# A graph layer on one core: sets of two units in a new order, 24 groups gathered wholly by TensorE, h's bf16 parts made by TensorE

## The chip, the core and the metric

One core of a Trainium2 chip. The metric is the device time of one execution in microseconds (us). The profile has one execution, with TensorE as PE (matmuls) and PEld (its weight loads), VectorE as DVE, ScalarE as ACT, GpSimd as POOL and the queues of DMA issues on SyncE as SPq.

## The reference: what is computed

```python
h = relu(layernorm(x))                       # x: 6250 nodes x 64
msg = relu(h[src] + edge_attr)               # 206250 edges x 64
agg = segment_sum(msg, dst, 6250)            # dst is sorted
out = x + (relu((h + agg) @ W1 + b1) @ W2 + b2)
```

The edges hold every drawn pair in both directions and one loop for each node, ordered by their destination.

## The kernel before

**Groups.** The 206250 edges are cut into 268 groups of 768 (6 columns of 128 edges) and a last, smaller one, numbered 268. Groups 0 to 4 are gathered wholly by GpSimd (`gather`, L204: one indirect DMA for each column of 128 rows). In the others GpSimd gathers three columns, and TensorE finds h for the other three; 12 groups (`WHOLE`) are found wholly by TensorE, in two halves. Three columns found by TensorE are a *unit*: 276 units, two to a *set*, 138 sets, and three sets to a round of ranks (46 rounds).

**How TensorE gathers.** h stands in SBUF as `hp`, 128 partitions x 49 rows x three bf16 parts x 64, whose sum is h. For each set the edges are sorted into places, at most 32 for each of 24 lists. `find` (L465, VectorE) compares the list of node numbers with each partition's number and writes `found`, a 0/1 matrix, in three comparisons (two over 1536 elements, one over 256). `slots_of` (L497, TensorE) multiplies `hp` by it, 52 matmuls of 128x32 weights for a unit, into three PSUM banks `half`, two columns of lists to a bank; `slots_out` (L506, ScalarE) copies a bank to `picked` in bf16. `back` (L484, VectorE; its last block by ScalarE, `back_far` and `back_near`, L474 and L477, as abs and relu of a difference) makes the 0/1 matrix `backs`, six blocks of 128x768 for a set. `pick` (L513, TensorE) multiplies it, 18 matmuls of 128x128 for a unit, and adds up in one of two `pick` banks, into which `room` (L522, ScalarE) has copied the unit's edge attributes.

**The rest of a unit.** `messages` adds the gathered columns (L597, VectorE), sums the three parts out of the `pick` bank (L600, VectorE) and applies relu (L602, ScalarE). `one_hot` (L581, VectorE) makes the matrix from each edge to the 32 destinations of the group's window. `window_sum` (L612, TensorE) multiplies the two, fp32, 128x64 weights, and `sum_into_z` (L575, VectorE) adds the result to z, which is transposed. Its column comes out of a register, loaded for 16 groups at a time by `window_start` (L442). `blocks_behind` starts the two matmuls with W1 and W2 (L631, L642) for every block of 512 nodes that is finished.

**Ranks.** The places come from counting: `rank_at` (L280, VectorE), `rank_count` (L285 and L287, TensorE, and L291, ScalarE), `rank_of` (L295 to L301, VectorE), `rank_marks`, `rank_turn` (L325, TensorE, L327, ScalarE), `rank_holds`, `rank_fits`, `source` (L339, TensorE, L344, ScalarE). The lists go to DRAM and come back to all partitions (`source_load`, `spot_load`).

**The order** is written by hand; nothing is rescheduled, each engine works through its instructions as `half(u)` and the code around it issue them. In `half(u)` a unit has TensorE's window sum of the unit before, the slots of the next set, and the pick of the next unit; then VectorE's and ScalarE's work, and one step of the ranks at certain units. Gathers of GpSimd wait for listed matmuls (`beats`), so that they come in time and not earlier.

**The start.** The layer norm goes through h in four pieces (`ln_head`, `ln_rows`), stores the rows for the gathers, and transposes them into z (`ln_turn`, L386, TensorE, L387, ScalarE). `ln_parts` makes the three parts of `hp` later, in steps that are put between the first groups' norms by `fill`: a cast by ScalarE (L392), a difference by VectorE (L394), a cast (L395), a difference (L397). `places` computes part and place numbers for all edges (L264 to L273, VectorE); `slots_of_edges` (L745 to L756) needs a matmul that spreads `base` (L747). Groups 0 to 2 are gathered from x itself and normed by `norm_edges` (L545 to L556).

## Time and profile before

| | |
|---|---|
| median of 3 runs (all) | 1082.63 us (1082.12, 1082.63, 1085.3) |
| profiled execution, its time | 1080.78 us |
| profiled execution, its span | 1079.1 us |
| mean granted TensorE clock | 0.974 |

The span reaches from the first to the last instruction; 1.7 us of the execution lie around it. Busy time counts an engine's own work, and a matmul's end has its drain in it, so successive matmuls overlap in the rows. "Idle before" is the engine's idle time in front of an instruction, with what ended it behind the arrow.

### The profile page before, as it was taken

To read this page: it belongs to the slowest core of one execution; us is meant where nothing else is said; L and a number is where in the kernel's file an instruction comes from. 1 tells how busy PE (TensorE), PEld (TensorE's weight loads), DVE (VectorE), ACT (ScalarE), POOL (GpSimd) and SP (SyncE) were. 2 spreads that over 40 slices of the span, in tenths; PEclk is the share of its full clock that TensorE was granted. 3 is DMA by queue.
4 is the path that set the end of the run, shared out by engine and by line. 5 is a ranking of instruction groups with operands and counts; after the bars stand their busy time and mean duration, and the time that the engine had idled before them with its cause. 6 is when DMAs were issued, how large, how long until landed. Compare 5 with 4: busy or idle time off the path is not lost.

```text
span 1079.1 us, 55140 instructions
## 1 busy us (share of the span) xinstructions
PE 994.9 (92%) x23185; PEld 865.5 (80%) x23185; DVE 960.5 (89%) x2686; ACT 940.6 (87%) x1979; POOL 793.9 (74%) x798
## 2 busy tenths in 40 slices
PE   3159999999999999999999999999999999999997
PEld 2148888888878888888888888888888888888885
DVE  8869889898998998998999898998999898998984
ACT  6459889899989998898998998998998998998985
POOL 7677777777777777777777777777777777777740
PEclk9659999999999999999999999999999999999998
DMA  6445566565655665665665656565656665655650
GB/s 207 126 117 150 164 164 187 141 178 158 188 143 150 180 190 143 170 169 165 163 174 149 184 157 165 155 199 156 161 148 187 164 170 154 185 158 161 167 132 10
DMA packets 115098, 172.36 MB, mean 160 GB/s; under 512 B 28444, under 2 KB 83613, under 8 KB 114845
## 3 DMA queue, kind: packets, MB, share of 16 engines
q1 hardware_dynamic: 89752, 143.03, 43.7%
q0 software_dynamic: 25088, 25.74, 13.5%
q8 instruction: 184, 3.01, 1.1%
q14 instruction: 70, 0.57, 0.2%
q10 hardware_dynamic: 4, 0.01, 0.0%
HBM read 164.85 MB, written 3.84 MB: 156 GB/s over the span
## 4 chain that ended last, share of the span: by engine, by line
PE 76%; DVE 10%; issue 5%; DMA 4%; ACT 3%; POOL 1%; DVEq 1%; SPq 0%; ACTq 0%
PE pick L513 34%; PE half L497 26%; PE half L612 10%; DVE backs L484 2%; DVE found L465 2%; DVE ea L600 2%; DMA xg<-h_rows,src_sb 2%; PE rows L339 2%; PE rows L642 1%; PE rows L631 1%; PE rows L287 1%; POOL xr L204 1%; DMA x<-in_x_dram 1%; DVE oh L581 1%; PE rows L285 1%
## 5 line engine op out<-in xcount | busy, mean ns | idle before, releaser
L204 POOL DMA_INDIRECT xg<-h_rows,src_sb x754 | 759.4, 1007 | 231.6 <-issue 105.2
L513 PE MATMUL pick<-picked,backs 128*128 128x192 bf16 x4968 | 459.9, 247 | 1.1 <-ACT pick L522 1.1
L513 PEld LDWEIGHTS <-backs 128*128 128x128 bf16 x4968 | 397.5, 98 | 45.1 <-issue 43.6
L506 ACT CAST picked<-half 128x384 bf16<-128x384 f32 x828 | 370.4, 480 | 54.3 <-PE half L497 47.2
L497 PE MATMUL half<-hp,found 128*32 128x192 bf16 x14352 | 352.8, 248 | 7.5 <-DVE found L465 4.9
L497 PEld LDWEIGHTS <-found 128*32 128x32 bf16 x14352 | 286.6, 97 | 22.2 <-issue 5.1
L484 DVE TENSOR_SCALAR backs<-spots,ids 128x768 bf16<-128x768 int16 x690 | 255.8, 419 | 0.0
L600 DVE TENSOR_REDUCE ea<-pick 128x192 f32<-128x576 f32 x276 | 206.8, 749 | 21.6 <-PE pick L513 19.7
L465 DVE TENSOR_SCALAR found<-sources,nodes_of 128x1536 bf16<-128x1536 int16 (+1 forms) x414 | 206.1, 525 | 0.1
L612 PEld LDWEIGHTS half<-oh,msg 128*64 128x64 f32 x3224 | 121.7, 138 | 62.0 <-issue 27.4
L522 ACT COPY pick<-ea 128x576 f32<-128x576 f32 x264 | 170.4, 646 | 0.0
L612 PE MATMUL half<-oh,msg 128*64 128x32 f32 x3224 | 152.4, 227 | 13.5 <-DVE z L575 10.8
L602 ACT ACTIVATE msg<-ea 128x384 f32<-128x384 f32 (+2 forms) x281 | 146.3, 521 | 10.7 <-DVE ea L600 7.2
L477 ACT ACTIVATE backs<-dist,ones 128x768 bf16<-128x768 bf16 x138 | 131.7, 954 | 0.3 <-ACT dist L474 0.3
L474 ACT ACTIVATE dist<-spots,far 128x768 bf16<-128x768 int16 x138 | 131.4, 952 | 0.0
L575 DVE TENSOR_TENSOR z<-z,half 128x32 f32 x281 | 50.9, 181 | 73.2 <-ACT picked L506 43.5
L581 DVE TENSOR_TENSOR oh<-slot,slots 128x192 f32<-128x192 int16 (+2 forms) x281 | 94.5, 336 | 1.0 <-PE half L612 1.0
L597 DVE TENSOR_TENSOR ea<-ea,xg 128x192 f32<-128x192 f32 x252 | 87.4, 347 | 0.7 <-issue 0.7
L285 PE MATMUL rows<-at,upper 128*128 128x432 f16 x46 | 16.4, 358 | 21.7 <-DVE at L280 19.7
L339 PE MATMUL rows<-holds,marks 128*96 128x96 f16 x276 | 25.8, 231 | 11.4 <-DVE holds L313 5.0
L291 ACT CAST before<-rows 128x432 f16<-128x432 f32 x46 | 23.9, 519 | 14.3 <-PE rows L287 14.3
L344 ACT CAST source<-rows 24x64 int16<-24x64 f32 x138 | 28.1, 203 | 9.5 <-PE rows L339 4.4
(107 smaller groups left out, 435.1 us busy)
## 6 DMA issues: line engine op xcount, KB each, us to landing
sources<-source_row SPq DMA_DIRECT2D x138, 384.0 KB
ea<-in_edge_attr_dram SPq DMA_DIRECT2D x268, 192.0 KB
spots<-spot_rows SPq DMA_DIRECT2D x138, 192.0 KB
xg<-h_rows,src_sb POOLq DMA_INDIRECT x754
xb<-in_x_dram SPq DMA_DIRECT2D x12, 128.0 KB
out_dram<-o SPq DMA_DIRECT2D x12, 128.0 KB
h_rows<-x SPq DMA_DIRECT2D x3, 384.0 KB
dst_sb<-in_dst_main_dram SPq DMA_DIRECT2D x1, 804.0 KB
```

The costliest lines, as they stand in the source:

```text
L204: it = nc.gpsimd.indirect_dma_start(out=xg[:, j, :], out_offset=None, in_=rows[:, :], in_offset=bass.IndirectOffsetOnAxis(ap=idx[:, j:j + ...
L465: nc.vector.tensor_scalar(found[k][:, b * PARTS:b * PARTS + n].rearrange("p m i s -> p (m i s)"), sources[k][:, :n * 2 * S], nodes_of[:, b ...
L474: nc.scalar.activation(dists[k], spots[k].bitcast(I16), AF.Abs, bias=far)
L477: nc.scalar.activation(backs[k][:, Q - 1].rearrange("p t s -> p (t s)"), dists.pop(k), AF.Relu, bias=ones[:, 0:1], scale=-1.0)
L484: nc.vector.tensor_scalar(backs[k][:, q].rearrange("p t s -> p (t s)"), spots[k].bitcast(I16), ids[:, q:q + 1], None, op0=ALU.is_equal)
L497: last = nc.tensor.matmul(ps[j * S:(j + 1) * S, u], found[k][:, m, i, :], hp[:, min(m, RR - 1)].rearrange("p t d -> p (t d)"), start=(b == ...
L506: nc.scalar.copy(picked[k][:, n0:n0 + 2], halves.pop((k, n0)))
L513: last = nc.tensor.matmul(ps[:, u, :3].rearrange("p t d -> p (t d)"), backs[k][:, q, i * H + u, :], picked[k][:, i * Q + q], start=False, ...
L522: nc.scalar.copy(picks[u][:, :H, :3], parts)
L600: nc.vector.tensor_reduce(ea[:, c0:c0 + H], picks.pop(u)[:, :H, :3].rearrange("p j t d -> p j d t"), AX.X, ALU.add)
L602: nc.scalar.activation(msg[:, lo:hi], ea[:, lo:hi], AF.Relu)
L612: last = nc.tensor.matmul(pa[i * D:(i + 1) * D], msg[:, j, :], oh[:, j, :], start=(j < lo + 2), stop=(j >= hi - 2))
```

## The change

- **Groups.** Every eleventh group from the tenth on is found wholly by TensorE: 24 for 12. There are 288 units, 144 sets, 48 rounds.
- **Order.** `half(u)` now differs for the first and the second unit of a set. The first issues the window sum, three banks of slots, the pick; the second the pick, three banks of slots, the window sum. The window sum of unit u-1 and that of u therefore follow each other on TensorE, and so do two picks (with a step of the ranks, or a result block, between them). `slots_out` directly follows each bank's slots. Both `sum_into_z` of a set stand in the first half, and the second `room` is issued there too. The steps of the ranks start one unit earlier.
- **Comparisons.** The third comparison of `found` is made by ScalarE (abs, then relu). The last block of `backs` is made by ScalarE for every other set and by VectorE for the rest; its two steps follow each other.
- **h's parts.** For each piece of the norm, TensorE multiplies h by the identity (fp32) and adds minus the first part (bf16) in a `pick` bank, ScalarE casts that to the second part; TensorE adds minus the second part, ScalarE casts the third. The transposes into z follow behind all pieces.
- **Smaller ones.** `code` is gone, its numbers are in `part`; the casts of `own` for all later rounds go to ScalarE, inside the norm; the norms of groups 0 to 2 go step by step for all three; `rank_of` of the third round is made in the start.

```diff
 F0 = 5
 SETS = 3
 RG = 2 * SETS
-HEAD, PERIOD = 2 * RG - 1, 4 * RG - 1
-assert (NG + 1 - F0 - HEAD) % PERIOD == 0
-WHOLE = [F0 + RG - 1] + list(range(F0 + HEAD + 2 * RG - 1, NG + 1, PERIOD))
+HEAD = PERIOD = 2 * RG - 1
+assert (NG + 1 - F0) % PERIOD == 0
+WHOLE = list(range(F0 + RG - 1, NG + 1, PERIOD))
 UNITS = []
 for g in range(F0, NG + 1):
     UNITS.append((g, G - H))
...
+    from_b = const.tile([P, PARTS, H], F16, name="from_b")
+    nc.gpsimd.iota(from_b, pattern=[[1, PARTS], [0, H]], base=BIAS // STEP, channel_multiplier=0,
+                   allow_small_or_imprecise_dtypes=True)
+    less_b = const.tile([P, P], BF16, name="less_b")
+    nc.vector.tensor_scalar_mul(less_b, ident, -1.0)
...
     def stretches(t_sb, c0, c1):
-        n, g0 = (HEAD, F0) if c0 == 0 else (PERIOD, F0 + HEAD + (c0 - 2) // 4 * PERIOD)
+        n, g0 = (HEAD, F0) if c0 == 0 else (PERIOD, F0 + c0 // 2 * PERIOD)
...
-    def places(c0, c1):
+    def places_own(c0, c1):
+        n = c1 - c0
+        own = lnp.tile([P, n, CC], F32, name="own", bufs=1)
+        m, parts = stretches(src_sb, c0, c1)
+        for src, w, gs in parts:
+            to = own.rearrange("p c s -> p (c s)").rearrange("p (e w g j) -> p e w g j", w=2, g=m, j=H)[:, :, w, gs]
+            if c0 == 0:
+                nc.vector.tensor_copy(to, src)
+            else:
+                nc.scalar.copy(to, src)
+        return own
+
+    def places(c0, c1, own):
         n = c1 - c0
         row = lnp.tile([P, n, CC], I16, name="row", bufs=1)
         off = lnp.tile([P, n, CC], F32, name="off", bufs=1)
         second = lnp.tile([P, n, CC], I16, name="second", bufs=1)
         third = lnp.tile([P, n, CC], F32, name="third", bufs=1)
-        own = lnp.tile([P, n, CC], F32, name="own", bufs=1)
-        m, parts = stretches(src_sb, c0, c1)
-        for src, w, gs in parts:
-            nc.vector.tensor_copy(own.rearrange("p c s -> p (c s)")
-                                  .rearrange("p (e w g j) -> p e w g j", w=2, g=m, j=H)[:, :, w, gs], src)
...
-        nc.vector.scalar_tensor_tensor(part[:, c0:c1], off, float(RR), third, op0=ALU.add, op1=ALU.add)
-        nc.vector.tensor_scalar(code[:, c0:c1], part[:, c0:c1], float(STEP), float(BIAS), op0=ALU.mult, op1=ALU.add)
+        nc.vector.scalar_tensor_tensor(part[:, c0:c1], off, float(RR + BIAS // STEP), third, op0=ALU.add, op1=ALU.add)
...
-        nc.vector.tensor_tensor(spot_i[c], ranks[c], code[:, c], ALU.add)
+        nc.vector.scalar_tensor_tensor(spot_i[c], part[:, c], float(STEP), ranks[c], op0=ALU.mult, op1=ALU.add)
...
                 nc.tensor.transpose(pt[:, u, :], h[:, i + u, :], ident[:PP, :PP])
             nc.scalar.copy(zv[:, :, r + i:r + i + n], pt[:, :n].rearrange("d u p -> d p u"))
-    def ln_parts(r, m, h):
+    def pieces(i, r, m):
+
+        flat = pick_banks[i % 2].rearrange("p j t d -> p (j t d)")
+        for a in range(0, m, 8):
+            b = min(a + 8, m)
+            yield flat[:, a * D:b * D], slice(a, b)
+
+    def mid_piece(i, r, m, h):
         hv = hp[:, r:r + m]
-        rest = lnp.tile([PP, m, D], F32, name="rest")
         nc.scalar.copy(hv[:, :, 0], h)
-        yield
-        nc.vector.tensor_tensor(rest, h, hv[:, :, 0], ALU.subtract)
-        nc.scalar.copy(hv[:, :, 1], rest)
-        yield
-        nc.vector.tensor_tensor(hv[:, :, 2], rest, hv[:, :, 1], ALU.subtract)
+        for ps, rows_of in pieces(i, r, m):
+            nc.tensor.matmul(ps, ident, h[:, rows_of].rearrange("p r d -> p (r d)"), start=True, stop=False)
+            nc.tensor.matmul(ps, less_b, hv[:, rows_of, 0], start=False, stop=True)
+        flat = pick_banks[i % 2].rearrange("p j t d -> p (j t) d")
+        nc.scalar.copy(hv[:, :, 1], flat[:, :m])
+
+    def low_piece(i, r, m, h):
+        hv = hp[:, r:r + m]
+        for ps, rows_of in pieces(i, r, m):
+            nc.tensor.matmul(ps, less_b, hv[:, rows_of, 1], start=False, stop=True, skip_group_check=True)
+        flat = pick_banks[i % 2].rearrange("p j t d -> p (j t) d")
+        nc.scalar.copy(hv[:, :, 2], flat[:, :m])
     def combine(xg, ea, n):
         nc.vector.tensor_tensor(xg[:, :n], xg[:, :n], ea[:, :n], ALU.add)
...
         nc.sync.dma_start(out=spots[k], in_=spot_rows[k * 2 * H:(k + 1) * 2 * H, :]
                           .rearrange("(o t) s -> o (t s)", o=1).to_broadcast([P, 2 * H * P]))
+    last_node = const.tile([P, 1], F32, name="last_node")
+    nc.vector.tensor_scalar_mul(last_node, nodes_of[:, BB:], -1.0)
+
     def find(k, b):
         if b == 0:
             found[k] = hot.tile([P, PARTS * BB + J, 2, S], BF16, name="found")
         n = PARTS if b < BB else J
-        nc.vector.tensor_scalar(found[k][:, b * PARTS:b * PARTS + n].rearrange("p m i s -> p (m i s)"),
-                                sources[k][:, :n * 2 * S], nodes_of[:, b:b + 1], None, op0=ALU.is_equal)
+        to = found[k][:, b * PARTS:b * PARTS + n].rearrange("p m i s -> p (m i s)")
+        if b < BB:
+            nc.vector.tensor_scalar(to, sources[k][:, :n * 2 * S], nodes_of[:, b:b + 1], None, op0=ALU.is_equal)
+        else:
+            dist = rank.tile([P, J * 2 * S], BF16, name="dist", bufs=1)
+            nc.scalar.activation(dist, sources[k][:, :n * 2 * S], AF.Abs, bias=last_node)
+            nc.scalar.activation(to, dist, AF.Relu, bias=ones[:, 0:1], scale=-1.0)
     far = const.tile([P, 1], F32, name="far")
     nc.vector.tensor_scalar_mul(far, ids[:, Q - 1:], -1.0)
-    dists = {}
+
+    def is_shared(k):
+        return k > 1 and k % 2 == 1
     def back_far(k):
-        dists[k] = rank.tile([P, 2 * H * P], BF16, name="dist", bufs=1)
-        nc.scalar.activation(dists[k], spots[k].bitcast(I16), AF.Abs, bias=far)
-
-    def back_near(k):
-        nc.scalar.activation(backs[k][:, Q - 1].rearrange("p t s -> p (t s)"), dists.pop(k), AF.Relu,
-                             bias=ones[:, 0:1], scale=-1.0)
+        to = backs[k][:, Q - 1].rearrange("p t s -> p (t s)")
+        apart = rank.tile([P, 2 * H * P], BF16, name="apart", bufs=1)
+        nc.scalar.activation(apart, spots[k].bitcast(I16), AF.Abs, bias=far)
+        nc.scalar.activation(to, apart, AF.Relu, bias=ones[:, 0:1], scale=-1.0)
+
+    def back_begin(k):
+        backs[k] = hot.tile([P, Q, 2 * H, P], BF16, name="backs")
     def back(k, q0, q1):
-        if q0 == 0:
-            backs[k] = hot.tile([P, Q, 2 * H, P], BF16, name="backs")
-        for q in range(q0, min(q1, Q - 1)):
+        if q0 == 0 and k not in backs:
+            back_begin(k)
+        for q in range(q0, min(q1, Q - is_shared(k))):
             nc.vector.tensor_scalar(backs[k][:, q].rearrange("p t s -> p (t s)"), spots[k].bitcast(I16),
                                     ids[:, q:q + 1], None, op0=ALU.is_equal)
         if q1 == Q:
...
-    def norm_edges(xg):
-        s = work.tile([P, G], F32, name="raw_s")
+    raw = {}
+
+    def raw_head(g):
+        xg = taken[g][1]
+        s = work.tile([P, G], F32, name="raw_s", bufs=RAW)
         nc.vector.tensor_reduce(s, xg, AX.X, ALU.add)
         nc.vector.tensor_scalar_mul(s, s, 1.0 / D)
         nc.vector.tensor_tensor(xg, xg, s.unsqueeze(2).to_broadcast([P, G, D]), ALU.subtract)
         sq = work.tile([P, G, D], F32, name="msg", bufs=3)
         nc.scalar.activation(sq, xg, AF.Square)
-        fill()
-        v = work.tile([P, G], F32, name="raw_v")
+        raw[g] = s, sq
+
+    def raw_var(g):
+        v, sq = raw[g]
         nc.vector.tensor_reduce(v, sq, AX.X, ALU.add)
         nc.scalar.activation(v, v, AF.Sqrt, bias=eps_sb, scale=1.0 / D)
-        fill()
+
+    def raw_rows(g):
+        xg, v = taken[g][1], raw.pop(g)[0]
         nc.vector.reciprocal(v, v)
         nc.vector.scalar_tensor_tensor(xg, xg, 0.0, v.unsqueeze(2).to_broadcast([P, G, D]),
                                        op0=ALU.max, op1=ALU.mult)
...
+    def slots_by(k, n0s):
+        for n0 in n0s:
+            last = slots_of(k, n0)
+            slots_out(k, n0)
+            if n0 != n0s[1]:
+                beats.append(last)
+
     def half(u):
         g = group_of(u)
         k, i = divmod(u, 2)
-        first = ((0, 2), (6, 8))[i]
-        later = ((4,), (10,))[i]
-        now = is_set(k + 1)
         if is_first(u):
             enter(g + AHEAD, beats[-G + H:])
+        if is_set(k + 3):
+            if i == 0:
+                source_load(k + 3)
+            else:
+                spot_load(k + 3)
         if i == 0:
-            if is_set(k + 3):
-                source_load(k + 3)
-        elif is_set(k + 3):
-            spot_load(k + 3)
-        window_sum(u - 1)
-        if u + 1 < U:
+            window_sum(u - 1)
             room(u + 1)
-        if now:
-            for n0 in first:
-                begun = slots_of(k + 1, n0)
-                slots_out(k + 1, n0)
-                if n0 == first[0]:
-                    beats.append(begun)
-            for n0 in later:
-                beats.append(slots_of(k + 1, n0))
-        if u + 1 < U:
+            if is_set(k + 1):
+                slots_by(k + 1, (0, 2, 4))
             beats.append(pick(u + 1, range(H)))
-        messages(u)
-        if now:
-            for n0 in later:
-                slots_out(k + 1, n0)
-        one_hot(u)
-        if i == 0:
+            messages(u)
+            if u + 2 < U:
+                room(u + 2)
+            one_hot(u)
+            for v in (u - 2, u - 1):
+                sum_into_z(v)
+                blocks_behind(v)
             if is_set(k + 1):
-                back_near(k + 1)
                 back(k + 1, 3, Q)
-            sum_into_z(u - LAG)
-            blocks_behind(u - LAG)
             if is_set(k + 2):
                 find(k + 2, 0)
                 find(k + 2, BB)
+                if is_shared(k + 2):
+                    back_begin(k + 2)
+                    back_far(k + 2)
         else:
-            if is_set(k + 2):
-                back_far(k + 2)
-                find(k + 2, 1)
-            sum_into_z(u - LAG)
-            blocks_behind(u - LAG)
+            if u + 1 < U:
+                beats.append(pick(u + 1, range(H)))
+            messages(u)
+            if is_set(k + 1):
+                slots_by(k + 1, (6, 8, 10))
+            window_sum(u - 1)
+            one_hot(u)
             if is_set(k + 2):
                 back(k + 2, 0, 3)
-        chunk(u + 14, rank_at)
-        chunk(u + 13, rank_count)
-        chunk(u + 12, rank_of)
-        chunk(u + 11, rank_marks)
-        chunk(u + 11, rank_turn)
-        chunk(u + 10, rank_holds)
-        chunk(u + 10, rank_fits)
-        chunk(u + 9, source)
+                find(k + 2, 1)
+        chunk(u + 15, rank_at)
+        chunk(u + 14, rank_count)
+        chunk(u + 13, rank_of)
+        chunk(u + 12, rank_marks)
+        chunk(u + 12, rank_turn)
+        chunk(u + 11, rank_holds)
+        chunk(u + 11, rank_fits)
+        chunk(u + 10, source)
         if g in CHECKS and is_first(u):
             find_left(CHECKS.index(g))
-
...
         if len(heads) > 1:
             rows.append(ln_rows(*heads[-2]))
         if len(rows) > 1:
-            ln_turn(*rows[-2])
+            low_piece(len(rows) - 2, *rows[-2])
+        if rows:
+            mid_piece(len(rows) - 1, *rows[-1])
         if r == CUTS[1]:
             rank_turn(0)
             source(0)
+        if r == CUTS[3]:
+            own = places_own(2, NCH)
     rows.append(ln_rows(*heads[-1]))
-    ln_turn(*rows[-2])
-    split = [ln_parts(*r) for r in rows]
+    low_piece(len(rows) - 2, *rows[-2])
+    mid_piece(len(rows) - 1, *rows[-1])
+    low_piece(len(rows) - 1, *rows[-1])
+    for row in rows:
+        ln_turn(*row)
     nc.sync.dma_start(out=w1_sb[:D], in_=w1)
     nc.sync.dma_start(out=w1_sb[D:], in_=w1)
     nc.sync.dma_start(out=w2_sb, in_=w2)
     nc.sync.dma_start(out=b1_sb, in_=b1.rearrange("(d o) -> d o", o=1))
     nc.sync.dma_start(out=b2_sb, in_=b2.rearrange("(o d) -> o d", o=1).to_broadcast([P, D]))
     slots_of_edges()
-    ln_turn(*rows[-1])
     rank_fits(0)
     for g in range(F0 + 2):
         enter(g)
-    places(2, NCH)
+    places(2, NCH, own)
     for k in (0, 1):
         source_load(k)
         spot_load(k)
     banks_begin()
+    for step in (raw_head, raw_var, raw_rows):
+        for g in range(RAW):
+            step(g)
     for g in range(F0):
         for i in range(g * LOOK // F0, (g + 1) * LOOK // F0):
             tails_begin(i)
...
+        if g == 4:
+            rank_of(2)
...
-    while split:
-        fill()
-    back_far(0)
-    back_near(0)
```

21 lines of the change are left out of this document (6 added, 15 removed).

## The prediction

> **What bounds the kernel now.** I read the page first, then the 100 us windows, then the groups by shape, then the timeline of one stretch of 15 us. The page has four engines nearly full; the second line is its chain of work that ended last.
>
> ```profile
> PE 994.9 (92%) x23185; PEld 865.5 (80%) x23185; DVE 960.5 (89%) x2686; ACT 940.6 (87%) x1979; POOL 793.9 (74%) x798
> ...
> PE 76%; DVE 10%; issue 5%; DMA 4%; ACT 3%; POOL 1%; DVEq 1%; SPq 0%; ACTq 0%
> ```
>
> A full engine need not be the bound. The window from 200 to 300 us (busy time in the order PE, PEld, DVE, ACT, POOL, then the granted clock) and the groups by shape (busy time, mean ns, idle time before them and who ended it) say which one is.
>
> ```profile
> 200.00:300.00 100.00, 97.96 (x2336) 85.51 (x2332) 91.91 (x260) 91.64 (x194) 76.09 (x77) 1.00 0.62 167
> ```
> ```profile
> L204 POOL DMA_INDIRECT xg<-h_rows,src_sb x754 | 759.4, 1007 | 231.6 <-issue 105.2 <-PE half L497 55.7 <-PE pick L513 16.5
> L513 PE MATMUL pick<-picked,backs 128*128 128x192 bf16 x4968 | 459.9, 247 | 1.1 <-ACT pick L522 1.1
> ...
> L506 ACT CAST picked<-half 128x384 bf16<-128x384 f32 x828 | 370.4, 480 | 54.3 <-PE half L497 47.2 <-DVE at L280 1.4 <-DVE found L465 0.7
> L497 PE MATMUL half<-hp,found 128*32 128x192 bf16 x14352 | 352.8, 248 | 7.5 <-DVE found L465 4.9 <-issue 2.4
> ...
> L484 DVE TENSOR_SCALAR backs<-spots,ids 128x768 bf16<-128x768 int16 x690 | 255.8, 419 | 0.0
> ...
> L612 PE MATMUL half<-oh,msg 128*64 128x32 f32 x3224 | 152.4, 227 | 13.5 <-DVE z L575 10.8 <-ACT backs L477 1.1 <-ACT source L344 0.7
> ...
> L597 DVE TENSOR_TENSOR ea<-ea,xg 128x192 f32<-128x192 f32 x251 | 87.2, 347 | 0.7 <-issue 0.7
> ```
>
> TensorE's three main groups stood idle for 1.1, 7.5 and 13.5 us in the whole run, and ScalarE waited 47.2 us for TensorE. GpSimd issues its gathers end to end (759.4 busy and 231.6 of short gaps, about 1.3 us for each of 754), but VectorE's addition that uses them (L597) waited 0.7 us in all, so they arrive in time. **TensorE is the bound.** Its rows in the stretch (start, duration with the drain, instruction) give the prices, always from one start to the next:
>
> ```profile
> 502.29 1.66 PE L513 MATMUL pick<-picked,backs 128*128 128x192 bf16 x18
> 503.79 0.56 PE L339 MATMUL rows<-holds,marks 128*96 128x96 f16 x6
> 504.27 0.54 PE L612 MATMUL half<-oh,msg 128*64 128x32 f32 x12
> 504.74 1.26 PE L497 MATMUL half<-hp,found 128*32 128x192 bf16 x52
> 505.93 1.66 PE L513 MATMUL pick<-picked,backs 128*128 128x192 bf16 x18
> 507.52 0.54 PE L612 MATMUL half<-oh,msg 128*64 128x32 f32 x12
> ...
> 509.18 1.66 PE L513 MATMUL pick<-picked,backs 128*128 128x192 bf16 x18
> 510.68 0.35 PE L285 MATMUL rows<-at,upper 128*128 128x432 f16 x1
> 510.86 0.47 PE L287 MATMUL rows<-at,ones_b 128*128 128x288 f16 x2
> 511.26 0.42 PE L612 MATMUL half<-oh,msg 128*64 128x32 f32 x6
> 511.61 1.26 PE L497 MATMUL half<-hp,found 128*32 128x192 bf16 x52
> ```
>
> A unit is window sum (W) 0.47, slots (S) 1.19, pick (P) 1.59: 3.25 us, 6.50 a set of two. The 138 sets make 897 us of the 1079.1 us span. The pick takes 1.59 ahead of a window sum (505.93 to 507.52), but 1.50 ahead of matmuls over 128 or 96 columns (509.18 to 510.68, 502.29 to 503.79). So a change of column width (128, 64, 32) costs about 0.095 us.
>
> **The change part by part.** *TensorE, steady part.* The order of a set was W S P W S P, six width changes; it becomes W S P P S W, where the next set's W follows at once: four. A set is then 6.50 - 2 x 0.095 = 6.31 us. The neighbours P-S and S-W are not in the trace. Each is bounded by 0 and by twice 0.095; I take 0.095, what the nearest row, P-W, shows. But 12 more groups are split in two, so there are 288 units for 276: 144 x 6.31 - 138 x 6.50 = **+11.5 us**. The matmuls of the ranks now stand between two picks: L339 cost a unit 1.50 + 0.48 for 1.59, 0.39 more, and L285 with L287 1.50 + 0.58 for 1.59, 0.49; that stays. L325 (128 by 18) has a width change on each side instead of one: 0.25, estimated from 0.06 of streaming, for 0.16. With two more rounds of three sets: 48 x 1.13 - 46 x 1.04 = +6.4. A window sum over three columns costs 0.35 (511.26 to 511.61) for 0.47 over six, so a group in two parts costs some 0.13 more there, 12 times: +1.6. Together **+19**.
>
> *Gathers.* 36 fewer, some 47 us of GpSimd's queue. Nobody waits for it (0.7 us), so 0.
>
> *VectorE.* Half a comparison more a set on average for `backs` (0.37 each: 255.8 over 690), and the third comparison of `found`, a third of the size, goes to ScalarE: between -0.18 and +0.19 a set, and I take 0. It works 91.91 in 100 us; a set with its ranks is 6.50 + 0.35 or longer, so 6.3 or a little more. TensorE will need 6.31 + 0.38 = 6.69. That covers VectorE by 0.2 to 0.4 us a set; each 0.1 us beyond it would cost 14 us.
>
> *ScalarE.* Its rows in the same stretch:
>
> ```profile
> 500.08 0.96 ACT L477 ACTIVATE backs<-dist,ones 128x768 bf16<-128x768 bf16 x1
> 500.92 0.66 ACT L522 COPY pick<-ea 128x576 f32<-128x576 f32 x1
> 501.80 0.86 ACT L506 CAST picked<-half 128x384 bf16<-128x384 f32 x2 [0.23 <-PE half L497]
> 502.55 0.54 ACT L602 ACTIVATE msg<-ea 128x384 f32<-128x384 f32 x1
> 502.98 0.48 ACT L506 CAST picked<-half 128x384 bf16<-128x384 f32 x1
> ...
> 504.38 0.64 ACT L344 CAST source<-rows 24x64 int16<-24x64 f32 x3
> ...
> 511.37 0.52 ACT L291 CAST before<-rows 128x432 f16<-128x432 f32 x1 [0.32 <-PE rows L287]
> 511.78 0.65 ACT L522 COPY pick<-ea 128x576 f32<-128x576 f32 x1
> 512.35 0.86 ACT L506 CAST picked<-half 128x384 bf16<-128x384 f32 x2
> ```
>
> From start to start: copy of a bank 0.38, message 0.43, start of a pick bank (`room`) 0.57, a step of the comparison 0.84; a rank copy 0.2 to 0.6, mean 0.37. A bank is ready about 0.70 behind its first slots. I lay the new queue out, from the set's second slots at 0. TensorE: W at 1.19 and 1.57, S 2.04, P 3.23, ranks 4.73, P 5.10, next set 6.69. ScalarE: copies from 0.70, `room` 1.84, copies from 2.74, message 3.88, second `room` 4.31 to 4.96, 0.14 ahead of the pick at 5.10. Then comes `found` (two steps of 256 elements, 0.8, estimated between nothing and two steps of 0.96), in every second set the last block of `backs` (0.96, a wait for that result, 0.84), 0.37 for the rank copy and 0.43 for a message. So after such a set ScalarE is free at 8.3, while the next bank is ready at 6.69 + 0.70 = 7.4. The message is late for its window sum by up to 0.2, and what is left of the delay makes the second `room` of the next set end 0.28 after TensorE wants it. A pair of sets loses between 0 and 0.48; I take 0.28, since the 0.2 hangs on the 0.8 alone: 72 x 0.28 = **+20** (0 to +35).
>
> The Trainium skill, TensorEngine Tiling (Array Packing), section PSUM Bottleneck, warns that tiling speeds up TensorE but not the copies out of PSUM, and advises to share them between ScalarE and VectorE. The 47.2 us that ScalarE spent waiting for TensorE speak against it before the change; by the rule the term just worked out is not 0 after it.
>
> *The start.* Rows of TensorE, of VectorE and of ScalarE:
>
> ```profile
> 15.91 2.77 PE L386 MATMUL half<-ident,x 128*64 128x128 f32 x12 [0.55 <-DVE x L372]
> ...
> 25.21 1.47 PE L386 MATMUL half<-ident,x 128*64 128x128 f32 x12 [1.86 <-ACT z L387]
> ```
> ```profile
> 26.61 0.96 DVE L372 SCALAR_TENSOR_TENSOR x<-x,ln_v 128x768 f32<-128x768 f32 x1
> ...
> 28.92 1.83 DVE L748 SCALAR_TENSOR_TENSOR slot<-dst_sb,rows 128x1608 int16<-128x1608 int32 x1 [0.87 <-PE rows L747]
> ...
> 47.58 0.96 DVE L394 TENSOR_TENSOR rest<-x,hp 128x768 f32<-128x768 f32 x1 [0.17 <-ACT hp L392]
> ...
> 68.27 1.34 DVE L465 TENSOR_SCALAR found<-sources,nodes_of 128x1536 bf16<-128x1536 int16 x3
> ```
> ```profile
> 26.22 1.68 ACT L387 COPY z<-half 64x512 f32<-64x512 f32 x3
> ```
>
> From L748 at 28.92 to `found` at 68.27 VectorE is the path, 39.4 us. Eight passes for h's parts leave it (0.96 each), so do `code` and the casts of `own` (together one or two passes) and a few waits for ScalarE between them; one `rank_of`, about a pass, moves in. I make it 29 us. But the parts now stand inside the norm: on ScalarE, the square root of piece i+1 is queued behind both casts of piece i, and the second cast waits for its matmuls. By the transposes 128 columns of fp32 take 0.21 us in a slow phase of TensorE (15.91) and 0.11 in a fast one (25.21); for a product in fp32 I double it, and with the bf16 part a piece takes 1.9 to 3.8 us. With three pieces in a chain the last h comes 8 to 12 us later than 26.61. Behind it stand the last parts (4 to 7 us) and now all 13 copies into z (1.68 for three, 7 in all), and only then the matmul that L748 waits for. L748 starts at 46 to 53 and `found` at 75 to 82: +7 to +14, and about +4 if each estimate falls on its low side. I take **+8**, nearer to the fast rows, because TensorE is busier here than it was.
>
> *Stalls that go.* TensorE's waits behind z (10.8) have a cause on VectorE that stays; where ScalarE holds TensorE up anyway, they coincide: **-5** (0 to -12).
>
> **Sum.** 1080.78 (the profiled execution: 1079.1 span and 1.7 around it) + 19 + 20 + 8 - 5 = 1122.8. The median of the three runs is 1.85 above that execution; I put **1123**.
>
> **Rivals.** (1) *TensorE stays the only bound* and ScalarE keeps up. For it: its wait of 47.2 us until now. 1080.8 + 19 + 8 - 5 = 1103 (1086 to 1108, with the start at its low end and more stalls gone). (2) *ScalarE and VectorE become the bound.* For it: a cover of 0.1 to 0.3 us a set. With 0.48 a pair (35), 0.1 a set on VectorE (14) and the start at +11: 1080.8 + 19 + 35 + 14 + 11 - 5 = 1155 (1136 to 1160). (3) *Faster: the two unseen width changes cost nothing.* Place: P-S and S-W, 288 in all; price 0.095 each, 27 us. With ScalarE keeping up and the stalls gone: 1080.8 + 19 - 27 + 8 - 12 = 1069. The point: without a hold by ScalarE the sum is +22, so it is faster only if a change costs less than 0.02. Against it: the one change that a row isolates costs 0.095. The Trainium skill's TensorEngine Tiling (Array Packing), section Key Properties, says that changing the tiling mode drains TensorE; by that rule both cost like the others, and (3) is unlikely. (4) *The change doesn't do what it is worth most for*: if gathers were the bound after all, 36 fewer would give up to 47 us, but TensorE then ends it at 1080.8 + 19 + 8 - 22 (all idle time of its groups) = 1086. The 0.7 us of L597 speak against it; it lies within the next case.
>
> **Chances.** My forecast (1108 to 1136) 0.45; (1) 0.24; (2) 0.11; (3) 0.13, 1060 to 1079; close to no change, with (4), 0.07. About 0.3%, 3.2 us, is what a measurement of this kernel can tell from none. Faster 0.13, same 0.07, slower 0.80. The range 1080 to 1142 leaves out (3) and the upper part of (2).
>
> **What will show it.** Right: pick to pick 1.50, pick to slots 1.59 and slots to window sum 1.19; 6.31 us a set where nothing waits; in every second set picks that wait for `room`; L748's counterpart starting at 46 us or later and the first pick past 78 us. Wrong: picks that never wait for ScalarE (then 1); pick to slots at 1.50 (then 3); VectorE without idle time (then 2); a first pick ahead of 75 us, which takes the start's term to nothing or below.

## The result, and the profile after

| | before | after |
|---|---|---|
| median of 4 runs each | 1083.97 us | 1205.86 us |
| range | 1082.12 to 1086.61 | 1201.45 to 1210.89 |
| profiled execution, its time / span | 1080.78 / 1079.1 us | 1210.89 / 1209.1 us |
| mean granted TensorE clock | 0.974 | 0.950 |

After against before: ratio 1.1124, 95% interval 1.1073 to 1.1175. The kernel became 122 us slower; the forecast was 1123 us, some 40 slower.

The page after: busy time by engine, the chain that ended last (by engine), and the groups that answer to those shown of before.

```profile
PE 1055.5 (87%) x24077; PEld 913.7 (76%) x24077; DVE 995.0 (82%) x2702; ACT 995.4 (82%) x2222; POOL 756.8 (63%) x763
...
PE 49%; ACT 27%; DVE 12%; issue 7%; DVEq 2%; DMA 2%; POOL 1%; ACTq 0%; SPq 0%; POOLq 0%
...
L549 PE MATMUL pick<-picked,backs 128*128 128x192 bf16 x5184 | 499.5, 251 | 28.1 <-DVE backs L520 24.7 <-ACT pick L558 1.8
...
L542 ACT CAST picked<-half 128x384 bf16<-128x384 f32 x864 | 359.3, 484 | 79.5 <-PE half L533 69.6
L533 PE MATMUL half<-hp,found 128*32 128x192 bf16 x14976 | 373.7, 251 | 3.8 <-DVE found L495 2.4
...
L651 PE MATMUL half<-oh,msg 128*64 128x32 f32 x3224 | 127.9, 227 | 55.1 <-ACT picked L542 52.5
...
L616 DVE TENSOR_TENSOR z<-z,half 128x32 f32 x293 | 54.7, 187 | 145.2 <-ACT picked L542 52.5
```

ScalarE's share of the chain went from 3% to 27%. TensorE's window sums (L651) stood idle 52.5 us for ScalarE's copies out of the slots' banks, where before they stood 13.5 in all, most of it for z; its picks (L549) stood 24.7 us for `backs`, where before they stood 1.1. No engine is full any more: all four big ones have lower shares than before. The window from 200 to 300 us, in the columns of the one shown before, has TensorE at 89.29 for 97.96 and the granted clock at 0.95 for 1.00:

```profile
200.00:300.00 100.00, 89.29 (x2055) 77.97 (x2056) 80.69 (x220) 81.34 (x184) 62.74 (x62) 0.95 0.54 145
```

A pair of sets in the steady part, TensorE and ScalarE (start, duration, instruction, idle time before it):

```profile
500.70 1.26 PE L533 MATMUL half<-hp,found 128*32 128x192 bf16 x52
...
501.89 0.89 PE L651 MATMUL half<-oh,msg 128*64 128x32 f32 x24
...
502.71 1.26 PE L533 MATMUL half<-hp,found 128*32 128x192 bf16 x52
...
503.90 1.66 PE L549 MATMUL pick<-picked,backs 128*128 128x192 bf16 x18
...
504.47 0.55 ACT L641 ACTIVATE msg<-ea 128x384 f32<-128x384 f32 x1
...
505.86 1.67 PE L549 MATMUL pick<-picked,backs 128*128 128x192 bf16 x18
...
506.44 0.92 ACT L510 ACTIVATE apart<-spots,far 128x768 bf16<-128x768 int16 x1
...
507.39 0.94 ACT L511 ACTIVATE backs<-apart,ones 128x768 bf16<-128x768 bf16 x1
507.46 1.26 PE L533 MATMUL half<-hp,found 128*32 128x192 bf16 x52
...
508.63 0.52 ACT L641 ACTIVATE msg<-ea 128x384 f32<-128x384 f32 x1
...
509.05 1.23 ACT L542 CAST picked<-half 128x384 bf16<-128x384 f32 x3
...
509.57 0.89 PE L651 MATMUL half<-oh,msg 128*64 128x32 f32 x24 [0.86 <-ACT picked L542]
```

The first set shows the prices that were forecast: slots to window sum 1.19 (500.70 to 501.89), slots to pick 1.19, pick to slots 1.60 (505.86 to 507.46). In the second set ScalarE makes the last block of `backs` (506.44 to 508.33), so the next message starts at 508.63 and the first copy of the bank at 509.05. TensorE finished its slots 1.19 after 507.46, at 508.65, and its window sum came 0.92 later, at 509.57, half a microsecond into the copies. The row at 509.57 holds two sums, 12 matmuls each. The first, which waited, multiplies the message made at 504.47, long ready; the one at 508.63 is for the second. What the first waited for is the copy: the result of a window sum lies in the bank of the unit's first slots (`pa`, L648, columns 384 and up), and it started when the copy of that bank's other columns was done.

This short stop did not lower the clock: from 505 to 517 us, with this wait in it, the granted clock stayed 1.00. From 280 to 286 us, behind a pick that waited 2.92 us, it was 0.50.

### The profile page after: what moved, and what is told of

It is laid out like the page before. It is cut to its first block, busy times and chain, and to the rows that moved or that the text cites. A ratio compares the mean times of both kernels' runs of the same rounds, so it can differ in the third digit from the quotient of the medians.

```text
span 1209.1 us, 56795 instructions
## 1 busy us (share of the span) xinstructions
PE 1055.5 (87%) x24077; PEld 913.7 (76%) x24077; DVE 995.0 (82%) x2702; ACT 995.4 (82%) x2222; POOL 756.8 (63%) x763
## 4 chain that ended last, share of the span: by engine, by line
PE 49%; ACT 27%; DVE 12%; issue 7%; DVEq 2%; DMA 2%; POOL 1%; ACTq 0%; SPq 0%; POOLq 0%
PE pick L549 18%; PE half L533 17%; PE half L651 9%; ACT picked L542 7%; ACT apart L510 4%; ACT msg L641 4%; ACT backs L511 3%; DVE backs L520 3%; ACT pick L558 2%; DVEq L467 2%; ACT dist L498 2%; DVE ea L639 2%; DVE found L495 1%; PE rows L681 1%; PE rows L670 1%
## 5 line engine op out<-in xcount | busy, mean ns | idle before, releaser
L209 POOL DMA_INDIRECT xg<-h_rows,src_sb x718 | 724.1, 1009 | 380.0 <-PE half L533 149.8
L549 PE MATMUL pick<-picked,backs 128*128 128x192 bf16 x5184 | 499.5, 251 | 28.1 <-DVE backs L520 24.7
L549 PEld LDWEIGHTS <-backs 128*128 128x128 bf16 x5184 | 432.3, 100 | 67.4 <-DVE backs L520 33.5
L520 DVE TENSOR_SCALAR backs<-spots,ids 128x768 bf16<-128x768 int16 x793 | 301.5, 431 | 3.1 <-DMA spots<-spot_rows 3.0
L641 ACT ACTIVATE msg<-ea 128x384 f32<-128x384 f32 (+1 forms) x293 | 148.3, 506 | 53.1 <-DVE ea L639 49.7
L495 DVE TENSOR_SCALAR found<-sources,nodes_of 128x1536 bf16<-128x1536 int16 x288 | 177.3, 616 | 0.0
L651 PE MATMUL half<-oh,msg 128*64 128x32 f32 x3224 | 127.9, 227 | 55.1 <-ACT picked L542 52.5
L651 PEld LDWEIGHTS half<-oh,msg 128*64 128x64 f32 x3224 | 111.2, 140 | 85.1 <-ACT picked L542 80.7
L616 DVE TENSOR_TENSOR z<-z,half 128x32 f32 x293 | 54.7, 187 | 145.2 <-ACT picked L542 52.5
L622 DVE TENSOR_TENSOR oh<-slot,slots 128x192 f32<-128x192 int16 (+1 forms) x293 | 96.5, 329 | 9.0 <-PE half L651 7.8
L499 ACT ACTIVATE found<-dist,ones 128x256 bf16<-128x256 bf16 x144 | 73.2, 508 | 4.7
L498 ACT ACTIVATE dist<-sources,last_node 128x256 bf16<-128x256 int16 x144 | 74.5, 518 | 0.0
L511 ACT ACTIVATE backs<-apart,ones 128x768 bf16<-128x768 bf16 x71 | 66.4, 936 | 2.3
L510 ACT ACTIVATE apart<-spots,far 128x768 bf16<-128x768 int16 x71 | 65.3, 920 | 0.6 <-DMA spots<-spot_rows 0.6
L295 PE MATMUL rows<-at,upper 128*128 128x432 f16 x48 | 17.3, 360 | 27.7 <-DVE at L290 22.6
```

What stands on the lines that cost most here:

```text
L209: it = nc.gpsimd.indirect_dma_start(out=xg[:, j, :], out_offset=None, in_=rows[:, :], in_offset=bass.IndirectOffsetOnAxis(ap=idx[:, j:j + ...
L495: nc.vector.tensor_scalar(to, sources[k][:, :n * 2 * S], nodes_of[:, b:b + 1], None, op0=ALU.is_equal)
L510: nc.scalar.activation(apart, spots[k].bitcast(I16), AF.Abs, bias=far)
L511: nc.scalar.activation(to, apart, AF.Relu, bias=ones[:, 0:1], scale=-1.0)
L520: nc.vector.tensor_scalar(backs[k][:, q].rearrange("p t s -> p (t s)"), spots[k].bitcast(I16), ids[:, q:q + 1], None, op0=ALU.is_equal)
L549: last = nc.tensor.matmul(ps[:, u, :3].rearrange("p t d -> p (t d)"), backs[k][:, q, i * H + u, :], picked[k][:, i * Q + q], start=False, ...
```

## The experiments

The theory (A): the second window sum of a set waits for ScalarE's copy of the bank in which its own result lies; ScalarE is late there by the last block of `backs` in every second set; z, `backs` and the picks follow, and the clock falls in the stops (this last part was not tested by a run of its own). Rival (B): ScalarE and VectorE are full (995 us of work each), so what is won in one place is lost in the next. Rival (C): the 12 more groups broke the balance. Each time is compared with the kernel before, measured beside it on the same chip ("+75" is that difference); after stands at +122. Most of these are single runs, and four runs of the kernel after lie between 1201 and 1211 us, so a difference of 4 or 5 us between two of them tells nothing.

### VectorE makes every block of backs: +75

```diff
     def is_shared(k):
-        return k > 1 and k % 2 == 1
+        return False
```

> The kernel after, but VectorE makes all six blocks of backs in every set. Theory A (the second window sum of a set waits for ScalarE's copy of the bank in which its own result lies, and ScalarE is late by the last block of backs in every second set): the 59 us that TensorE lost between slots and window sum fall below 12, the half clock behind those stops goes with them (10 to 15 us), and VectorE pays 71 comparisons of 0.38 us, of which at most 20 us are seen: 1125 to 1155 us. Rival B (ScalarE and VectorE are simply full, 995 us of work each): the wait moves from window sums to the picks, which wait for backs; 1190 to 1225 us.

1156.92 us, +75.1: 47 less than after. The groups of the window sum and of the pick:

```profile
L549 PE MATMUL pick<-picked,backs 128*128 128x192 bf16 x5184 | 494.8, 249 | 29.7 <-DVE backs L520 25.0
...
L651 PE MATMUL half<-oh,msg 128*64 128x32 f32 x3224 | 128.9, 227 | 9.5 <-ACT picked L542 6.4
```

The window sum's wait fell from 52.5 to 6.4 us, as A has it; the picks' wait for `backs` stayed as it was (25.0), where B wanted it to grow. So it does not follow from the late sums either, as the theory had said. The time fell a little less than A said.

### The window sums in the bank that is copied second: +184

```diff
-        pa = half_banks[0][:, 2 * 3 * D + u % AB * W:][:, :W]
+        pa = half_banks[1][:, 2 * 3 * D + u % AB * W:][:, :W]
```

> The kernel after, but the window sums lie in the bank that is copied second among the three of a unit, not in the first. No engine has more or less to do. Theory A: the window sum waits for the next copy of ScalarE, up to 0.38 to 0.43 us later; in the 72 sets in which ScalarE is late that is up to +30 us, in the others a part of it: 1215 to 1245 us, with L651 waiting for picked 80 to 120 us in place of 52.5. Rival B (load alone) and rival C (the window sum waits for its message, which the profile's name of the releaser hides): 1198 to 1213 us, L651 as it was.

1265.39 us, +183.6. No instruction more, only another bank:

```profile
L651 PE MATMUL half<-oh,msg 128*64 128x32 f32 x3224 | 127.6, 227 | 106.2 <-ACT picked L542 104.3
```

The wait doubled, 52.5 to 104.3 us. So it is the copy, not the message and not the load. The time rose by even more than the bound given (1245): z, which reads the same bank, waits for the copies too, 120.9 us here for 52.5 in the kernel after.

### Comparisons ahead of z: +118, with the first edit too: +53

```diff
-            for v in (u - 2, u - 1):
-                sum_into_z(v)
-                blocks_behind(v)
             if is_set(k + 1):
                 back(k + 1, 3, Q)
...
                     back_far(k + 2)
+            for v in (u - 2, u - 1):
+                sum_into_z(v)
+                blocks_behind(v)
```

> The kernel after, but VectorE adds the two window sums into z behind the last blocks of backs and the comparisons of found, not ahead of them. Theory A': the pick waits inside for backs (33.9 us, 44 times) because z, which waits for the late window sum, and the register loads of 3.6 us stand ahead of backs; those waits fall below 10 us and with the clock the time falls by 25 to 40 us: 1165 to 1182 us; the waits of L651 for picked stay at 50 to 60. Rival B: VectorE is full, the waits return in another place: 1195 to 1215 us.

Alone: 1199.62 us, +117.8, only 4 less than after.

```profile
L549 PE MATMUL pick<-picked,backs 128*128 128x192 bf16 x5184 | 491.2, 250 | 2.3 <-ACT pick L558 1.5
...
L651 PE MATMUL half<-oh,msg 128*64 128x32 f32 x3224 | 127.0, 226 | 61.0 <-ACT picked L542 58.9
...
L681 PE MATMUL rows<-w_sb,h 64*128 64x64 f32 (+1 forms) x98 | 14.7, 293 | 26.0 <-ACT h L673 26.0
```

The picks' waits for `backs` are gone, as expected, and the expected 25 to 40 us did not come. The edit moved `blocks_behind` together with z, behind ScalarE's last block of `backs`, and the second matmul of a result block now waits for ScalarE's h 26.0 us for 9.7 in the kernel after; the window sums wait 6 us more (58.9 for 52.5). Without these two rows that looks like B. With both edits together, where ScalarE has no such block:

> The kernel after with both edits of the earlier runs: VectorE makes all blocks of backs (1156.92 alone), and z and the comparisons of found change places (1199.62 alone, its gain of 6 us hidden behind ScalarE's wait). Theory A: with ScalarE's wait gone, the picks' waits inside for backs (25 us for the matmuls, 36 for their weight loads, unchanged in the first of the two) are now on the path, and taking them away gives 20 to 35 us: 1120 to 1137 us. Rival B (VectorE is full, so what it does first does not matter): 1148 to 1160 us.

1134.39 us, +52.8: 22 less than with the first edit alone.

```profile
L549 PE MATMUL pick<-picked,backs 128*128 128x192 bf16 x5184 | 487.5, 250 | 2.0 <-ACT pick L558 1.8
...
L651 PE MATMUL half<-oh,msg 128*64 128x32 f32 x3224 | 128.3, 227 | 13.8 <-ACT picked L542 11.2
```

Now nothing takes the place of the waits for `backs` (the result blocks wait 9.7 us again). So they were a loss of their own, 22 us, and not a matter of how much VectorE works: in this run it makes 71 comparisons more. In the kernel after z stood ahead of the three comparisons that the next pick needs. VectorE waits there for ScalarE's copy of the bank in which the sums lie (52.5 us in 89 waits, 0.6 us each), for result blocks that read z (27.8 us in 11), and for the load of column numbers into registers, 17 times, 3.6 us each (the second line has the count, then the shortest, the median and the longest in ns):

```profile
DVE z L616 <- ACT picked L542: 52.5, 89, 1.2
```
```profile
L467 DVEq TENSOR_LOAD <-dst_sb x17: 2935/3607/3850, 74.6 to 1156.0; - x17
```

It is the loads that stopped the picks. All 15 places in which a pick waits for `backs` lie within 1.4 us of the end of one of them, such as this one, with its load from 275.8 to 279.5 us:

```profile
279.70 0.19 DVE L616 TENSOR_TENSOR z<-z,half 128x32 f32 x1 [3.50 <-issue]
```
```profile
280.27 2.75 PE L549 MATMUL pick<-picked,backs 128*128 128x192 bf16 x15 [2.92 <-DVE backs L520]
```

The kernel before has the same 17 loads, but there the comparisons stood ahead of z, and no pick waited for `backs`.

### The window sums further ahead: +230 and +109

First both window sums of a set behind the second pick (P P W W S S, three width changes), then the same a unit later, with the two edits above:

```diff
             if u + 1 < U:
                 beats.append(pick(u + 1, range(H)))
             messages(u)
+            one_hot(u)
+            window_sum(u - 1)
+            window_sum(u)
             if is_set(k + 1):
                 slots_by(k + 1, (6, 8, 10))
-            window_sum(u - 1)
-            one_hot(u)
```

> The kernel after, but both window sums of a set follow the second unit's pick, ahead of the slots (pick, pick, sum, sum, slots, slots), so that no sum stands behind a copy that was just asked for. All engines do the same work. Theory A: the waits of L651 for picked go (59 us), the clock comes back (10 to 15), and one width change of 0.095 us a set goes (14): 1110 to 1145 us, unless the second sum now comes too early for its message. Rival B (ScalarE and VectorE are full): the waits go elsewhere, 1190 to 1215 us.

> As the run with both edits, but the window sums of the two units before now follow the second unit's pick, one unit later than in the kernel after, so that no sum waits for a copy just asked for or for a message just made, and a set has three width changes. Theory A: L651 waits under 8 us in all, 0.095 us a set goes (14 us), 8 to 20 us below the run with both edits: 1100 to 1128 us. Rival B: a sum later by a unit makes z later, the slots wait for z, which reads the bank that they write: the same time or above it.

1311.67 us (+229.9) and 1190.91 (+109.3). Neither gained. In the first the sum's wait for the copy is gone, and it waits for its message instead, which now is what stands behind ScalarE's block:

```profile
L651 PE MATMUL half<-oh,msg 128*64 128x32 f32 x3224 | 145.9, 231 | 88.2 <-ACT msg L641 86.5
```

In the second the sums wait for no copy (6.7 us in all, for z), but the slots, no longer parted by sums, wait for `found`, and `one_hot` for its buffer:

```profile
L533 PE MATMUL half<-hp,found 128*32 128x192 bf16 x14976 | 380.1, 248 | 52.5 <-DVE found L495 49.7
...
L622 DVE TENSOR_TENSOR oh<-slot,slots 128x192 f32<-128x192 int16 (+1 forms) x293 | 97.8, 334 | 113.2 <-PE half L651 110.0
```

A's waits did go; its forecast of the time was wrong both times, because the new order made others.

### The groups alone, in the old order: +43

The kernel before with only the first hunk of the change (24 whole groups, `stretches` to match).

> The kernel before with one part of the change alone: 24 groups wholly by TensorE in place of 12, in the old order and with the old start. If TensorE's own work is what 12 more units cost: 12 x 3.25 us and two rounds of ranks, 1082 + 41 = 1118 to 1128 us, so more than a third of the whole loss. If the gathers had been the bound, 36 fewer would give time back: below 1082. If the groups were what broke the balance of the engines (ScalarE and VectorE late at the split groups): above 1140.

1124.27 us, +42.6, about what 12 units and two rounds of ranks take on TensorE (12 x 3.25 + 2 x 1.04 = 41). C falls.

### The old start: +110

The kernel after with `ln_parts` of before in its steps (`fill`) and the transposes in their old places:

```diff
-            low_piece(len(rows) - 2, *rows[-2])
-        if rows:
-            mid_piece(len(rows) - 1, *rows[-1])
+            ln_turn(*rows[-2])
...
-    for row in rows:
-        ln_turn(*row)
+    ln_turn(*rows[-2])
+    split = [ln_parts(*r) for r in rows]
```

> The kernel after, but the three parts of h are made as before (two casts by ScalarE and two differences by VectorE, in steps between the first groups' norms) and each piece is transposed inside the norm. If the later first pick (87.97 for 74.83 us) comes from h's parts standing inside the norm and the transposes behind it: first pick at 74 to 79 us, and the time 9 to 13 us lower, 1192 to 1199 us. If it comes from the other edits of the start (the casts of own, the norms step by step): first pick past 84 us, 1202 to 1210 us. If the start is hidden by what follows, the time stays although the first pick is early.

1191.23 us, +109.6: 12 less than after. Its first `found` and first pick in the timeline:

```profile
67.17 1.31 DVE L482 TENSOR_SCALAR found<-sources,nodes_of 128x1536 bf16<-128x1536 int16 x2
...
73.73 1.65 PE L536 MATMUL pick<-picked,backs 128*128 128x192 bf16 x18 [1.13 <-ACT pick L545]
```

And those of the kernel after:

```profile
81.28 1.32 DVE L495 TENSOR_SCALAR found<-sources,nodes_of 128x1536 bf16<-128x1536 int16 x2
...
87.97 3.04 PE L549 MATMUL pick<-picked,backs 128*128 128x192 bf16 x18 [1.13 <-ACT pick L558]
```

All of the late start was h's parts and the transposes behind them; nothing later hid it.

### Three mends: +22; with 12 whole groups -5

Both edits, the old start, and the second matmul of a result block in the other half of the set:

```diff
     def blocks_behind(u):
         g = group_of(u)
-        for c in sorted(res):
-            store(c, *res.pop(c))
-        for c in sorted(hid):
-            res[c] = result(c, *hid.pop(c))
         for c in range(NB):
...
+    def blocks_later():
+        for c in sorted(res):
+            store(c, *res.pop(c))
+        for c in sorted(hid):
+            res[c] = result(c, *hid.pop(c))
...
                 find(k + 2, 1)
+            blocks_later()
         chunk(u + 15, rank_at)
```

The four kernels of this part were first measured on a chip on which before took 1429 us; the last section has those times. On another chip:

> The same with 24 whole groups. If the losses are apart: 1134 - 15 - 12 = 1104 to 1112 us. If they share one cause (VectorE and ScalarE full, so that what is won in one place is lost in the next): 1118 to 1132 us.

1102.97 us, +21.7, as A has it and below B's range. TensorE's groups, and its window from 200 to 300 us:

```profile
L536 PE MATMUL pick<-picked,backs 128*128 128x192 bf16 x5184 | 479.2, 247 | 2.8 <-ACT pick L545 2.2 <-ACT picked L529 0.3
L520 PE MATMUL half<-hp,found 128*32 128x192 bf16 x14976 | 367.0, 248 | 8.4 <-DVE z L603 3.9 <-DVE found L482 2.4 <-issue 2.0
L638 PE MATMUL half<-oh,msg 128*64 128x32 f32 x3224 | 129.1, 226 | 14.0 <-ACT picked L529 11.6 <-DVE z L603 1.6 <-DVE ea L623 0.4
```
```profile
200.00:300.00 100.00, 96.99 (x2397) 86.35 (x2393) 94.14 (x262) 82.89 (x200) 73.89 (x74) 1.00 0.60 164
```

TensorE is nearly full again, with 96.99 of 100 us and a granted clock of 1.00; VectorE works 94.14 of 100 us beside it, and has 21% of the chain for 10% in the kernel before. In the kernel after, the two matmuls of a block stood in one half, and TensorE stopped for ScalarE's h, its matmuls 9.7 us and their weight loads 20.6:

```profile
L681 PE MATMUL rows<-w_sb,h 64*128 64x64 f32 (+1 forms) x98 | 13.8, 281 | 9.7 <-ACT h L673 9.7
```

In the run with the mends 0.4:

```profile
L668 PE MATMUL rows<-w_sb,h 64*128 64x64 f32 (+1 forms) x98 | 13.8, 281 | 0.4 <-ACT h L660 0.4
```

> The new order with 12 whole groups, VectorE making all blocks of backs, z behind the comparisons, the start of before, and a result block's two matmuls in different halves. If the groups cost the same in either order (43 us) and the losses are apart: 1061 to 1070 us, 1 to 2% below before (1082). If the gathers, 36 more, bind in the new order: 1075 us or above.

With 12 whole groups 1076.24 us; ratio to before 0.9949, interval 0.9934 to 0.9964: the only version below before, by 5 us where 11 to 20 were expected. 12 groups cost 27 us here, not 43. GpSimd's gathers have no stop longer than 0.3 us, from the first at 48.7 to the last at 1046.4 us. (Us in total, times, longest.)

```profile
POOL xg L209 <- issue: 91.5, 300, 0.3
POOL xg L209 <- PE half L520: 49.4, 162, 0.3
POOL xg L209 <- DMA xg<-h_rows,src_sb: 25.9, 85, 0.3
```

With 24 groups they do stop, up to 5.9 us:

```profile
POOL xg L209 <- PE pick L536: 42.3, 70, 5.9
```

So with 12 groups and the mends GpSimd has no room left. But that does not show it to be the bound: VectorE's addition that uses the gathers waited 0.3 us in all, for 0.7 in the kernel before. VectorE is the other candidate, with 34% of the chain:

```profile
PE 47%; DVE 34%; issue 7%; DMA 6%; ACT 4%; DVEq 1%; POOL 1%; SPq 0%; POOLq 0%; ACTq 0%
```

Which of them holds this version up stays open; a run with a number of groups between was not made.

> The kernel after with 12 whole groups and the start of before: the new order with ScalarE's comparisons alone. If the parts add up: 1191.23 - 43 = 1142 to 1155 us, so that order and comparisons alone cost 60 to 73 us. If it is the 12 more split groups that make ScalarE late: below 1120 us.

1158.27 us, +77.0: order and ScalarE's comparisons alone, 3 us above the range for parts that add up (C falls again).

> As e13b, and the window sums of the two units before follow the second pick (three width changes a set), the comparison of found for the second half is made ahead of the first three blocks of backs, and the matrices of the window sums have three buffers for two. If the waits for found and for that buffer were the whole loss of the later sums: 138 x 0.095 = 13 us below e13b, 1046 to 1062 us. If two runs of slots in one piece ask too much of ScalarE's copies (0.38 to 0.43 for a bank that TensorE fills in 0.40): the same as e13b or up to 15 us above.

The edits, beside the sums of the run a unit later:

```diff
-    oh = work.tile([P, G, W], F32, name="oh")
+    oh = work.tile([P, G, W], F32, name="oh", bufs=3)
...
+                find(k + 2, 1)
                 back(k + 2, 0, 3)
-                find(k + 2, 1)
```

1102.22 us, ratio to before 1.0196 (1.0161 to 1.0230): 26 above the run with mends and 12 groups, more than either side said. `found` and the buffer were mended and a loss remained: the picks stood idle 27.7 us for 4.5, mostly for `room`, which ScalarE makes behind the copies of two runs of slots that follow each other:

```profile
L536 PE MATMUL pick<-picked,backs 128*128 128x192 bf16 x4968 | 457.6, 246 | 27.7 <-ACT pick L545 15.8
```

### ScalarE's block in two steps: +108; with the mends +55

The second step goes to the second half of the set, behind its copies:

```diff
+    def back_near(k):
+        to = backs[k][:, Q - 1].rearrange("p t s -> p (t s)")
+        nc.scalar.activation(to, aparts.pop(k), AF.Relu, bias=ones[:, 0:1], scale=-1.0)
...
             if is_set(k + 2):
+                if is_shared(k + 2):
+                    back_near(k + 2)
                 back(k + 2, 0, 3)
```

> The kernel after, ScalarE's last block of backs as before in every second set, but its second step (0.94 us) stands behind the copies of the next half, not directly behind the first step. No engine has more or less to do. Theory A, by place: ScalarE is then late by 0.9 us less where the second window sum waits for its copy, L651's wait for picked falls from 52.5 to under 20 us and the time to 1150 to 1175 us (the waits for backs stay). By amount (rival B): the second step delays the next copies or the next room by as much, 1195 to 1212 us.

1187.13 us, +107.5: 14 less than after, between the two. The second sum's wait went from 52.5 to 7.7 us, the place at work, and a part came back as picks that wait for `room` (1.8 us in the kernel after, 13.7 in this run). TensorE's groups of this run:

```profile
L553 PE MATMUL pick<-picked,backs 128*128 128x192 bf16 x5184 | 491.2, 249 | 47.0 <-DVE backs L524 24.4 <-ACT pick L562 9.3 <-ACT pick L565 4.4
...
L655 PE MATMUL half<-oh,msg 128*64 128x32 f32 x3224 | 128.7, 227 | 10.9 <-ACT picked L546 7.7 <-DVE z L620 1.6 <-issue 0.4
```

> The run with the three mends and 24 groups (1102.97), with ScalarE's last block in every second set given back to it in two steps. VectorE has 71 comparisons fewer, 0.19 us a set, and ScalarE 0.93 us a set more. If VectorE holds that run up and the place is what cost: 1085 to 1100 us. If TensorE alone bounds it: 1100 to 1106 us. If ScalarE's amount costs: above 1115 us.

1134.66 us, +55.0: 33 above the same run without it, though VectorE has 71 comparisons less. So A in its pure form fell: of the 47 us that the block costs in the kernel after, its place explains the 14 that moving one step brought, and some 33 stay, as many as it costs in the mended run. There the picks stand idle 19.3 us for 2.8 and the window sums 18.3 for 14.0. That fits the prediction's layout, in which a set with the block has 0.9 us more of ScalarE's work than TensorE gives it time for; whether a third place would cost less wasn't tried.

## Why the prediction was wrong

It had the direction and the engine, and its time was 83 us low. Three steps of its sum failed: ScalarE's hold at +20, which measured +47; VectorE at 0, which measured +22; and the result blocks, for which it had no term, with some +19. The steps, by the runs (each is a difference between two of them, and the last row is what remains, so they add up to 122):

| step | forecast | measured |
|---|---|---|
| TensorE, steady part, with stalls that go | +19 - 5 = +14 | +21.7 (three mends) |
| ScalarE's hold | +20 (0 to +35) | +46.8 (75.1 for 121.9) |
| VectorE | 0 | +22.3 (52.8 for 75.1) |
| the start | +8 (+7 to +14) | +12.3 (109.6 for 121.9) |
| the result blocks | not in the sum | 52.8 - 21.7 - 12.3 = +18.8 |

- **TensorE.** Right in its prices. The unseen neighbours cost what the nearest row said: pick to slots 1.60 for 1.59, slots to window sum 1.19. Without a wait a set with ranks is 6.76 (500.70 to 507.46) for the forecast 6.31 + 0.49. With that, rival 3 (free width changes) falls. One small term has the wrong sign: 24 sums over three columns take 0.35 where the 6.31 counts 0.47, so -2.9 and not +1.6, and the sum of TensorE's terms would be +15 and not +19. No run takes apart why +21.7 was measured. The Trainium skill, TensorEngine Tiling (Array Packing), section Key Properties, says that changing the tiling mode drains TensorE. The trace agrees in so far as such changes took time: a pick takes 1.60 ahead of slots, for 1.50 ahead of matmuls of 128 columns.
- **ScalarE's hold: the first step that failed.** The queue had been laid out rightly (ScalarE free 0.9 after TensorE's next bank), but the prediction let TensorE feel it in two places, "the message is late for its window sum by up to 0.2" and a second `room` that ends 0.28 after TensorE wants it. TensorE stopped in a third. The picks, which were to wait for `room` in every second set, waited 1.8 us in the whole run. The window sum that waited, 0.86 in the set shown and 52.5 us in all, had its message; it waited for the copy behind the late one, because its result shares that copy's bank. What was missed is who else waits for that bank. This place is worth the 14 us that moving one step gave back. The other 33 us, which the same block costs in the run with the mends too, are 0.46 for each of 72 pairs: the top of the forecast's 0 to 0.48, for the 0.28 that was chosen.
- **VectorE at 0: the second.** Wrong in kind. The cover of 0.2 to 0.4 us a set was reckoned from amounts, and the amounts held: with 71 comparisons more VectorE still kept up. The order within its queue cost 22 us: 17 register loads of 3.6 us, which z needs, now stood ahead of comparisons that the next pick needed.
- **The start.** Right in its steps (L782 at 51.72, forecast 46 to 53; `found` at 81.28, forecast 75 to 82; first pick past 78), low in the choice: +8 was taken from +7 to +14. VectorE stood 13.2 us for one matmul behind 49 transposes:

```profile
38.13 0.40 DVE L779 CAST base<-dst_sb 1x269 f32<-1x269 int32 x1
51.72 1.83 DVE L782 SCALAR_TENSOR_TENSOR slot<-dst_sb,rows 128x1608 int16<-128x1608 int32 x1 [13.19 <-PE rows L781]
```
```profile
43.15 7.88 PE L398 MATMUL half<-ident,x 128*64 128x128 f32 x49
```

- **The result blocks: the third.** Not seen: both `blocks_behind` of a set now stand in one half, so the second matmul directly follows the first and waits for ScalarE between them. The 18.8 is what is left of the mends when the start is taken off, from single runs; the weight loads of those matmuls waited 20.6 us for ScalarE's h.
- **Gathers at 0.** Right for the kernel after. In the mended order 12 groups leave the gathers without a stop, and 36 fewer may be worth something there; that was argued from the trace and not shown.
- **The rivals.** (1), TensorE alone, 1103, has the time of the run with the mends (1102.97) by luck: that run has the old start, and its TensorE term is 8 us larger. (2), ScalarE and VectorE become the bound, came nearest, with a top of 1160: it added amounts, and most of the losses were waits. The Trainium skill, TensorEngine Tiling (Array Packing), section PSUM Bottleneck, warns that tiling does not speed up the copies out of PSUM. That bears on this case only in part: the sums did wait for such copies, but a copy took as long as before (484 ns for 480), and the comparison ahead of it made it late.

## What to carry to other kernels

When a queue is laid out by hand to find a late instruction, list for each consumer all that it waits for, the other readers of its PSUM bank too, and not only the operand that it multiplies; then look for the longest things in each in-order queue, register loads among them, and at what stands behind them. An engine's mean share says nothing of that. When an edit gives less than the wait that it takes away, look for the rows that grew before calling an engine full: the 25 us that one edit took from the picks came back mostly as 16 us at the result blocks, which it had moved along. Work shared out to an engine in every second stage must fit into that stage, not into the mean.
